# A GRU on one core: stores of the last steps regrouped, and the biases of the last two steps copied into PSUM by VectorE instead of multiplied in by TensorE

## The chip, the core and the metric

The kernel runs on one core of a Trainium2 chip. The metric is the device time of one execution in microseconds (us), lower is better. The core has a matrix engine (TensorE; PE in the profile, with PEld for its weight loads), VectorE (DVE), ScalarE (ACT), GpSimd (POOL) and SyncE (SP). Here SP does no arithmetic: it issues most of the transfers between device memory and the on-chip memory SBUF. Each engine works through its own list of instructions in the order in which the program wrote them; between engines, an instruction waits on semaphores until what it needs is done. Products are added up in PSUM, which is divided into banks of 512 float32 columns on 128 partitions; the kernel uses all eight.

## The reference, cut to what matters

A gated recurrent unit runs over T = 128 steps on a batch of B = 64 with width 512, and its outputs are added to the input:

```python
def step(h, inp):
    x_t, prop = inp
    comb = concatenate([x_t, h], -1)
    z = sigmoid(comb @ Wz + bz)
    r = sigmoid(comb @ Wr + br)
    h_cand = tanh(concatenate([x_t, r * h], -1) @ Wh + bh)
    h_new = (1.0 - z) * h + z * h_cand
    h_next = where(prop, tanh(h_new @ Wp + bp), h_new)   # every fourth step, not the last
    return h_next, h_new
out = x + ys
```

The x parts of the three products depend on no step, the h parts form a chain of 128 steps, and all is float32.

## The kernel before

**Two halves.** The batch is split into two halves of V = 32 rows (`S = 2`). `half(0)` and `half(1)` are generators that write the program; a loop at the end of the file takes turns between them by an estimated cost per product, and so the order of instructions on every engine is written out by that loop (`manual_schedule`: nothing is reordered later). In a step a half goes through its gates R, Z and H, each four units of two products (`gate`). A half's products use two of the four column groups of the matrix engine and 64 of the 128 PSUM partitions, so the two halves run beside each other. I call them lane 0 and lane 1: lane 0 works on partitions 0 to 63, lane 1 on 64 to 127. A step's chain in each lane is: R products, a sigmoid on ACT, `rh` and its transpose `rhT` on DVE, H products, a tanh on ACT, three DVE operations up to the transposed new state `hT`, and the next step's R products. While one of these waits is open, the matrix engine works on Z, on the other lane, and on units of a queue.

**The queue.** `put` appends units of work that is due later (the x products of coming steps), and `fill(n, h)` emits the next n units for lane h at a given place in the program (`PLACES`, `TAIL`, `AT_LAST` hold the counts). Lane 0 and lane 1 each walk the same list. A unit whose function returns `False` is not counted, and the next one is emitted in the same turn. When a list entry has an `end` function, it is called when lane 1 has passed it.

**The last two steps.** Steps T-2 and T-1 (`WIDE = 2`) are computed in another shape (`wide_step`): all x products and biases are added up beforehand in PSUM banks that the earlier method no longer needs, and the h products are added on top. `wide(t, i, h)` names 128 columns for a step, a gate and a half. For T-2 they lie in the banks `scratch_q` (R of both halves, Z of half 1) and `scratch_r` (Z of half 0, H of both); for T-1 in `scratch_a` (R of both, Z of half 1), `scratch_x` (Z of half 0) and `scratch_y` (H). At step T-10 the queue receives the x products of both steps (`wide_unit`, 12 units a step), a unit of bias products after each step's products (`wide_bias`, L595: 12 products for each lane, a 0/1 pattern `picks` times the bias in three bfloat16 parts, `thirds`) and `crossing_unit` (one unit that lane 0 computes for lane 1 and that ACT then copies over to partitions 64 to 127, L588). The first of these products to touch a bank starts the accumulation there.

**Where the units fall.** I follow the queue by hand from the counts: in step T-6 lane 0 emits its first `wide_unit` after `Z` unit 3 and the rest of R and the first two of Z, all of T-2, after its H products; step T-5 takes the rest of Z, H of T-2, the bias unit and the crossing; T-4 takes R and the first half of H of T-1; T-3 takes the rest of H, and Z; the last bias unit falls at the start of T-2 (`AT_LAST`: five units for lane 0, three for lane 1).

**Stores.** `behind_step` adds a step's state to `xr`, which holds four steps of x, on POOL (L968), and stores finished groups of four steps with eight transfers on SP (L978). For the last four steps, three are stored together behind step T-2 (`n = 3 if t == T - 2`), and the last step is stored by `wide_step`: half 0 with one transfer on SP (L1045), half 1 with four, two on SP and two on ACT (L1050).

Of the kernel before, what the change touches and what calls it, by code (L numbers as in the profile page):

```python
# [9 lines left out]
F32 = mybir.dt.float32  # L10
# [8 lines left out]
def kernel(  # L19
# [14 lines left out]
    nc = tc.nc  # L34
    B, T, D = x.shape
# [60 lines left out]
    def part(q):  # L96
        return slice(q * V, (q + 1) * V)
# [427 lines left out]
    def wide(t, i, h):  # L525
        if t == T - 1 and i == H_:
            return scratch[wide_banks(t, i)[0]][:, ts(h, J)]
        n, bank = divmod(ORDER.index((i, h)), 2)
        return scratch[wide_bank(t) + bank][:, ts(n, J)]

    def wide_banks(t, i):
        if t == T - 1 and i == H_:
            return (x_banks[1],)
        return wide_bank(t), wide_bank(t) + 1

    crossing = scratch[x_banks[1]][:, S * J :].rearrange("p (h j) -> p h j", h=S)

    def wide_products(t, i, h, lane, left, w, start=False):
        for c in range(2):
            q = 2 * lane + c  # L540
            nc.tensor.matmul(  # L541
                wide(t, i, h)[part(q)],
                lhsT=left,
                rhs=w[:, ts(q, J)],
                start=start,
                stop=True,
                skip_group_check=True,
            )
# [6 lines left out]
    def x_left(t, h, k):  # L555
        g, j = divmod(t, Q4)
        c0, s0 = divmod(k, C)
        return xT[g][:, j][:, c0, s0 * B + h * V : s0 * B + (h + 1) * V]

    def wide_unit(t, i, k):  # L560
        crossed_one = t == T - 1 and i == H_

        def unit(lane):
            if crossed_one and k == 0 and lane == 1:
                return False
            for h in range(S):
                start = not crossed_one and i != H_ and h == 0 and k == 0
                wide_products(t, i, h, lane, x_left(t, h, k), wx[:, k, i], start)

        return unit, S * J, wide_banks(t, i), None, ()  # L570

    def crossing_unit():
        def unit(lane):
            if lane == 1:
                return False
            for h in range(S):
                for c in range(2):
                    nc.tensor.matmul(
                        crossing[part(c), h],
                        lhsT=x_left(T - 1, h, 0),  # L580
                        rhs=wx[:, 0, H_, ts(2 + c, J)],
                        start=h == 0,
                        stop=True,
                        skip_group_check=True,
                    )

        def end():
            nc.scalar.copy(  # L588
                scratch[x_banks[1]][2 * V :, : S * J].rearrange("p (h j) -> p h j", h=S),
                crossing[: 2 * V],  # L590
            )

        return unit, S * J, (x_banks[1],), end, ()

    def wide_bias(t):  # L595
        def unit(lane):
            for i, row in ((R, 0), (H_, 1), (Z, 2)):
                for h in range(S):
                    for c in range(2):
                        q = 2 * lane + c  # L600
                        nc.tensor.matmul(
                            wide(t, i, h)[part(q)],
                            lhsT=picks[:, q],
                            rhs=thirds[:, row],
                            start=False,
                            stop=True,
                            skip_group_check=True,
                        )

        return unit, 192, wide_banks(t, R) + wide_banks(t, H_), None, ()  # L610

    MB = {}

# [240 lines left out]
    def begin(t):  # L854
        u = (t - 3) % 8
        even = FIRST + 2 * ((t - 3) // 8)
        if t == 1:
            put(batch((1, 0), [(1, 1), (1, 2)]))
        elif t == 2:
            put(batch((1, 1), [(1, 10), (1, 11)]) + batch((1, 2), [(1, 8), (1, 9)]))  # L860
        elif t == 3:
            put(batches(FIRST))
        elif u == 7:
            put(batches(even + 2))
        if t == T - 10:
            put(
                batch((LAST, 0), [(LAST - 1, 4), (LAST, 1)])
                + batch((LAST, 1), [(LAST, 2), (LAST, 10)])
                + [wide_unit(T - 2, i, k) for i in (R, Z, H_) for k in range(K)]
                + [wide_bias(T - 2), crossing_unit()]  # L870
                + [wide_unit(T - 1, i, k) for i in (R, H_, Z) for k in range(K)]
                + [wide_bias(T - 1)]
            )

    def behind_r(t, duo, u):
# [32 lines left out]
    def behind_step(t, duo, u, h_new):  # L908
        g, j = divmod(t, Q4)
        even, odd = FIRST + 2 * duo, FIRST + 2 * duo + 1  # L910
        if t == T - 7:
            pair_left(0, 1, 2, LAST)
            pair_right(0, 1, 10, LAST)
        if t == 0:
            sum_outer(2)
            sum_outer(4)
        if t == 3:
            pair_left(1, 8, 9)
            pair_right(1, 8, 11)

        if duo >= 0:
            if u == 0 and duo >= 1 and odd - 2 < LAST:
                outer_c22(odd - 2)
                outer_c21(odd - 2)
            if even * Q4 < T:
                if u == 0:
                    sum_s34(even)
                elif u == 1:
                    outer_1(even)
                    outer_c11(even)  # L930
                    sum_raw12(odd)
                elif u == 2:
                    sum_raw4(even)
                    outer_u1(even)
                    outer_5(even)
                elif u == 3:
                    outer_c12(even)
                    outer_u2(even)
                    outer_c22(even)
                    if odd < LAST:  # L940
                        sum_s12(odd)
                elif u == 4:
                    if odd < LAST:
# [12 lines left out]
        for i, v in ((0, kept_h[0]), (1, kept_h[1])) if t == 2 else ():  # L956
            o = xr[0][:, i].rearrange("p h (e k) -> p h e k", k=K)
            nc.gpsimd.tensor_add(o, o, v.rearrange("p h (k e) -> p h e k", k=K))
        if duo >= -1 and (even + 2) * Q4 < T:
            if t == 2 or (u == 6 and duo >= 0):  # L960
                sum_raw12(even + 2)
            if u == 7:
                sum_s12(even + 2)
        if t < 2:
            kept_h[t] = h_new
        if 2 <= t < T - 1:
            o = xr[g][:, j].rearrange("p h (e k) -> p h e k", k=K)
            nc.gpsimd.tensor_add(o, o, h_new.rearrange("p h (k e) -> p h e k", k=K))  # L968

        n = 0  # L970
        if t >= T - CHUNK:
            n = 3 if t == T - 2 else 0
        elif j == Q4 - 1:
            n = 4
        if n:
            for h in range(S):
                for q in range(NQ):
                    nc.sync.dma_start(  # L978
                        out=out[ts(h, V), t - n + 1 : t + 1, ts(q, J)],
                        in_=xr[g][part(q), j - n + 1 : j + 1, h, :],  # L980
                    )
# [12 lines left out]
    r_wide = rec[2][:, 1, 0]  # L994
# [6 lines left out]
    def wide_step(t, lane):  # L1001
# [8 lines left out]
        for i, h in ORDER:  # L1010
# [23 lines left out]
            else:  # L1034
# [7 lines left out]
                    continue  # L1042
                nc.vector.tensor_add(o, z_h, o)
                if h == 0:
                    nc.sync.dma_start(  # L1045
                        out=out[ts(h, V), t, :].rearrange("b (q n) -> q b n", q=NQ), in_=o
                    )
                else:
                    for q in (0, 2, 1, 3):
                        both_queues[q // 2].dma_start(out=out[ts(h, V), t, ts(q, J)], in_=o[part(q)])  # L1050

    def half(h):

# [159 lines left out]
```

## Time and profile before

| what | value |
|---|---|
| median of 3 runs | 1258.22 us (1257.46 to 1258.62) |
| the profiled execution, its own time | 1257.26 us |
| its span, first to last instruction | 1255.1 us |
| PE busy | 1247.5 us, 99% |
| DVE, ACT, POOL busy | 64%, 66%, 72% |
| granted TensorE clock, mean | 0.999 |

The profile gives times in us from the start of the span. L541 is line 541 of the kernel. An arrow in a group's name points from the operands to the result. A line of the timeline holds the start, the length, the engine, the line, the operation, the tiles and shapes, the number of instructions merged, and in brackets the idle time in front with the instruction that ended it. L246 is the line of all products of the usual steps, L541 of those of the last two steps, and L284 that of every transpose on DVE. A busy PE is not a measure of how full the array is: instructions of the two lanes overlap, and a record's length contains the way through the array.

### The profile page before, as it was taken

The page shows a single profiled execution, that of the slowest core. Times are in us where ns is not written, and L with a number is a line of the kernel's source. Part 1 is how long each engine was busy: PE and PEld are TensorE (multiplying, and loading weights), DVE is VectorE, ACT ScalarE, POOL GpSimd, SP SyncE. Part 2 cuts the span into 40 slices and gives each one's busy share as a digit, 9 for nine tenths or more (in the row PEclk, how much of TensorE's full clock was granted, in tenths as well). Part 3 has the DMA queues.
Part 4 walks back from the last instruction along what each step waited for, and adds up shares of the span by engine and source line. Part 5 has one row for each costly group of instructions (what it writes and reads, how often), then busy time and mean ns, then how long its engine had stood idle before and what let it go on. Part 6 is the DMA issues. An engine that isn't in the chain of part 4 may idle for free.

```text
span 1255.1 us, 61567 instructions
## 1 busy us (share of the span) xinstructions
PE 1247.5 (99%) x26384; PEld 1180.2 (94%) x26384; DVE 805.9 (64%) x2177; ACT 830.1 (66%) x2666; POOL 908.8 (72%) x1032
## 2 busy tenths in 40 slices
PE   9999999999999999999999999999999999999998
PEld 5999999999999999999999999999999999999987
DVE  5666666666666666666666666666666666666554
ACT  2566666666666676666666666666676666676663
POOL 4988777677876778767778677786777787677530
PEclk9999999999999999999999999999999999999999
DMA  7311112111121110121211211111211111111011
GB/s 249 91 38 40 49 36 53 40 50 42 31 53 52 38 51 24 51 54 37 53 31 41 53 47 43 36 49 41 54 37 46 44 37 53 43 48 36 9 35 33
DMA packets 112292, 61.14 MB, mean 49 GB/s; under 512 B 12776, under 2 KB 109300, under 8 KB 112020
## 3 DMA queue, kind: packets, MB, share of 16 engines
q1 hardware_dynamic: 111588, 56.90, 16.7%
q8 instruction: 208, 3.41, 1.1%
q14 instruction: 64, 0.52, 0.1%
q0 software_dynamic: 256, 0.14, 0.0%
q10 hardware_dynamic: 176, 0.16, 0.0%
HBM read 40.38 MB, written 16.78 MB: 46 GB/s over the span
## 4 chain that ended last, share of the span: by engine, by line
PE 98%; DMA 1%; SPq 0%; DVE 0%; issue 0%; ACT 0%
PE rec L246 44%; PE rec_z L246 16%; PE scratch_r L246 13%; PE scratch_q L246 10%; PE scratch_a L246 5%; PE scratch_y L246 4%; PE scratch_x L246 4%; DMA wx<-in_L_cond_Wh_dram 1%; PE scratch_a L541 0%; PE scratch_q L541 0%; PE scratch_r L541 0%; PE scratch_y L541 0%; SPq L127 0%; PE scratch_x L541 0%; SPq L141 0%
## 5 line engine op out<-in xcount | busy, mean ns | idle before, releaser
L246 PE MATMUL rec<-wh,rhT 128*32 128x256 f32 x4032 | 370.1, 379 | 0.0
L246 PE MATMUL rec<-wh,hT 128*32 128x256 f32 x3008 | 276.6, 379 | 0.0
L246 PE MATMUL rec_z<-wh,hT 128*32 128x256 f32 x3008 | 276.3, 379 | 0.0
L246 PEld LDWEIGHTS rec<-wh,rhT 128*32 128x32 f32 x4032 | 248.5, 110 | 15.8 <-ACT rec L442 0.3
L281 ACT ACTIVATE scratch_r<-rec 64x128 f32<-64x128 f32 x504 | 126.0, 250 | 128.7 <-PE rec L246 63.0
L442 ACT COPY rec<-cp 64x256 f32<-64x256 f32 x504 | 186.8, 371 | 20.2 <-DVE cp L483 1.0
L246 PEld LDWEIGHTS rec_z<-wh,hT 128*32 128x32 f32 x3008 | 191.6, 110 | 5.2
L246 PEld LDWEIGHTS rec<-wh,hT 128*32 128x32 f32 x3008 | 185.0, 110 | 10.4 <-issue 0.8
L281 ACT ACTIVATE rec_z<-rec_z 64x128 f32<-64x128 f32 x488 | 122.0, 250 | 91.1 <-PE rec_z L246 79.5
L281 ACT ACTIVATE c<-rec 64x128 f32<-64x128 f32 x504 | 136.7, 271 | 61.5 <-PE rec L246 50.4
L968 POOL TENSOR_TENSOR xr<-xr,h 128x256 f32<-128x256 f32 x125 | 109.2, 874 | 86.0 <-DVE h L1133 74.4
L711 POOL TENSOR_TENSOR cp<-mb,mb 128x768 f32<-128x768 f32 x76 | 139.0, 1829 | 9.3 <-DVE mb L677 5.6
L711 POOL TENSOR_TENSOR mb<-mb,mb 128x768 f32<-128x768 f32 x58 | 106.2, 1831 | 45.8 <-DVE mb L677 45.8
L711 POOL TENSOR_TENSOR cp<-mb 128x768 f32<-128x768 f32 x46 | 84.3, 1832 | 56.8 <-ACT rec_z L442 55.4
L246 PE MATMUL scratch_r<-tw,s 128*32 128x192 f32 x928 | 120.9, 326 | 0.0
L650 ACT COPY cq<-scratch_q 128x384 f32<-128x384 f32 x212 | 102.1, 482 | 19.5 <-PE scratch_q L246 18.0
L667 DVE TENSOR_TENSOR cx<-scratch_r,cx 128x384 f32<-128x384 f32 x106 | 59.1, 557 | 84.5 <-PE scratch_r L246 69.0
L246 PE MATMUL scratch_q<-tt,s 128*32 128x192 f32 x928 | 103.6, 326 | 0.0
L1097 DVE SCALAR_TENSOR_TENSOR keep<-rec_z,h 128x256 f32<-128x256 f32 x91 | 38.6, 424 | 95.6 <-ACT rec_z L281 86.2
L673 DVE TENSOR_TENSOR mb<-scratch_q,cx 128x384 f32<-128x384 f32 x106 | 59.0, 557 | 62.5 <-ACT cq L650 62.5
L1076 DVE TENSOR_TENSOR rh<-scratch_r,h 128x128 f32<-128x128 f32 x188 | 54.8, 292 | 58.9 <-ACT scratch_r L281 58.9
L246 PE MATMUL rec<-wp,hT 128*32 128x256 f32 x992 | 91.4, 379 | 0.0
(250 smaller groups left out, 3907.3 us busy)
## 6 DMA issues: line engine op xcount, KB each, us to landing
out_dram<-xr SPq DMA_DIRECT2D x249, 64.0 KB, 1.8
xr<-in_x_dram SPq DMA_DIRECT2D x248, 64.0 KB, 2.1
xs<-in_x_dram SPq DMA_DIRECT2D x240, 64.0 KB, 2.0
wx<-in_L_cond_Wz_dram SPq DMA_DIRECT2D x2, 512.0 KB, 7.0
wx<-in_L_cond_Wh_dram SPq DMA_DIRECT2D x2, 512.0 KB, 9.3
wh<-in_L_cond_Wr_dram SPq DMA_DIRECT2D x2, 512.0 KB, 8.3
wh<-in_L_cond_Wz_dram SPq DMA_DIRECT2D x2, 512.0 KB, 5.0
wh<-in_L_cond_Wh_dram SPq DMA_DIRECT2D x2, 512.0 KB, 8.3
```

Source lines behind the costliest of these rows:

```text
L246: nc.tensor.matmul(ps[part(2 * h + c)], lhsT=left, rhs=rhs(c), start=start, stop=True, skip_group_check=True,)
L281: nc.scalar.activation(o, v, func)
L442: nc.scalar.copy(gate_ps(i, h)[rows].rearrange("p d (c n) -> p d c n", c=C), G[t][rows, :, :, i, :].rearrange("p c d n -> p d c n"),)
L650: nc.scalar.copy(c[:, :nm], ps[:, :nm])
L667: nc.vector.tensor_add(T2[what][:, :nm], r_ps[:, :nm], T2[what][:, :nm])
L673: nc.vector.tensor_add(blocks(1, 1), runs(q_ps[:, :nm]), runs(T2[what][:, :nm]))
L711: nc.gpsimd.tensor_add(dst, a, b)
L968: nc.gpsimd.tensor_add(o, o, h_new.rearrange("p h (k e) -> p h e k", k=K))
L1076: nc.vector.tensor_mul(rh[:, h, :], r_, h_old[:, h, :])
L1097: nc.vector.scalar_tensor_tensor(out=kept[0], in0=kept[1], scalar=1.0, in1=kept[2], op0=ALU.subtract, op1=ALU.mult,)
```

## The change

Four things change.

1. **Biases of the last two steps.** At step 64, `load_bias_q` loads the biases br, bz, bh into SBUF tiles `bias_q`, each quarter spread over 32 partitions, with 12 transfers on SP. The bias products (`wide_bias`) go. Instead, queue entries `wide_seeds(t, i)` copy the bias of a gate into the PSUM columns of both halves with two VectorE copies (128 partitions by 128 columns; for H of T-1 only partitions 0 to 63). They are emitted when lane 0 reaches them, and count for nothing in the queue. All products then add to what is there (`start=False`).
2. **The order in the queue.** The seeds stand one gate ahead of their products; R and Z of T-2 stand together at the front. For H of T-1, four bias products in lane 1 remain (`crossing_bias`), and lane 0 skips that entry.
3. **The crossing.** Its two halves go to the last 128 columns of `scratch_y` and `scratch_a`, not both to `scratch_y`, and ACT copies them with two instructions instead of one.
4. **Stores.** Steps T-4 and T-3 are stored together behind T-3 with eight transfers; T-2 with one transfer for each half; of the last step, half 1 goes with one transfer on SP and one on ACT instead of two each.

```diff
@@ wide_unit, crossing_unit
-    crossing = scratch[x_banks[1]][:, S * J :].rearrange("p (h j) -> p h j", h=S)
+    crossing = [scratch[b][: 2 * V, 3 * J :] for b in (x_banks[1], a_bank)]
...
-                start = not crossed_one and i != H_ and h == 0 and k == 0
-                wide_products(t, i, h, lane, x_left(t, h, k), wx[:, k, i], start)
+                wide_products(t, i, h, lane, x_left(t, h, k), wx[:, k, i])
...
-            nc.scalar.copy(
-                scratch[x_banks[1]][2 * V :, : S * J].rearrange("p (h j) -> p h j", h=S),
-                crossing[: 2 * V],
-            )
-        return unit, S * J, (x_banks[1],), end, ()
-    def wide_bias(t):
+            for h in range(S):
+                nc.scalar.copy(wide(T - 1, H_, h)[2 * V :], crossing[h])
+        return unit, S * J, (x_banks[1], a_bank), end, ()
+    def load_bias_q():
+        for n in range(2):
+            tile_ = one.tile([P, S, J], F32, tag=f"h{n}", name=f"bias_q{n}")
+            for i in ((R, Z), (H_,))[n]:
+                bias_q[i] = tile_[:, i % 2]
+        for i, b in ((R, br), (Z, bz), (H_, bh)):
+            for q in range(NQ):
+                nc.sync.dma_start(
+                    out=bias_q[i][part(q)],
+                    in_=b.rearrange("(q o j) -> q o j", q=NQ, o=1)[q].broadcast_to([V, J]),
+                )
+    def wide_seeds(t, i):
         def unit(lane):
+            if lane == 0:
                 for h in range(S):
+                    rows = slice(0, 2 * V) if t == T - 1 and i == H_ else slice(None)
+                    nc.vector.tensor_copy(wide(t, i, h)[rows], bias_q[i][rows])
+            return False
+        return unit, 0, wide_banks(t, i), None, ()
+    def crossing_bias():
+        def unit(lane):
+            if lane == 0:
+                return False
+            for h in range(S):
+                for c in range(2):
+                    nc.tensor.matmul(wide(T - 1, H_, h)[part(2 + c)], lhsT=picks[:, 2 + c],
+                        rhs=thirds[:, 1], start=False, stop=True, skip_group_check=True)
+        return unit, 64, wide_banks(T - 1, H_), None, ()
@@ begin, at T - 10
-                + [wide_unit(T - 2, i, k) for i in (R, Z, H_) for k in range(K)]
-                + [wide_bias(T - 2), crossing_unit()]
-                + [wide_unit(T - 1, i, k) for i in (R, H_, Z) for k in range(K)]
-                + [wide_bias(T - 1)]
+                + [wide_seeds(T - 2, R), wide_seeds(T - 2, Z)]
+                + [wide_unit(T - 2, R, k) for k in range(K)]
+                + [wide_seeds(T - 2, H_)]
+                + [wide_unit(T - 2, Z, k) for k in range(K)]
+                + [wide_seeds(T - 1, R)]
+                + [wide_unit(T - 2, H_, k) for k in range(K)]
+                + [wide_seeds(T - 1, H_), crossing_unit()]
+                + [wide_unit(T - 1, R, k) for k in range(K)]
+                + [wide_seeds(T - 1, Z)]
+                + [wide_unit(T - 1, H_, k) for k in range(K)]
+                + [crossing_bias()]
+                + [wide_unit(T - 1, Z, k) for k in range(K)]
@@ behind_step
-            n = 3 if t == T - 2 else 0
+            n = 2 if t == T - 3 else 0
+            if t == T - 2:
+                for h in range(S):
+                    store_step(t, h)
...
+        if t == T // 2:
+            load_bias_q()
...
+    def store_step(t, h):
+        g, j = divmod(t, Q4)
+        nc.sync.dma_start(
+            out=out[ts(h, V), t, :].rearrange("b (q n) -> q b n", q=NQ), in_=xr[g][:, j, h, :]
+        )
@@ wide_step, the last step
-                    for q in (0, 2, 1, 3):
-                        both_queues[q // 2].dma_start(out=out[ts(h, V), t, ts(q, J)], in_=o[part(q)])
+                    for d in range(2):
+                        both_queues[d].dma_start(
+                            out=out[ts(h, V), t, ts(d, 2 * J)].rearrange("b (q n) -> q b n", q=2),
+                            in_=o[ts(d, 2 * V)],
+                        )
```

More of the change, by code (lines that the diff above doesn't have):

```diff
@@ L578, in unit @@
                     nc.tensor.matmul(
-                        crossing[part(c), h],
+                        crossing[h][part(c)],
                         lhsT=x_left(T - 1, h, 0),
                         rhs=wx[:, 0, H_, ts(2 + c, J)],
-                        start=h == 0,
+                        start=False,
                         stop=True,
@@ L587, in end @@
         def end():
[L588 to L595 removed]
+            for h in range(S):
+                nc.scalar.copy(wide(T - 1, H_, h)[2 * V :], crossing[h])
+        return unit, S * J, (x_banks[1], a_bank), end, ()
+    bias_q = {}
+    def load_bias_q():
[9 more added lines that the diff above has]
+                )
@@ L596, in unit @@
+    def wide_seeds(t, i):
         def unit(lane):
-            for i, row in ((R, 0), (H_, 1), (Z, 2)):
+            if lane == 0:
                 for h in range(S):
[L599 to L608, printed above, removed]
@@ L610, in wide_bias @@
-        return unit, 192, wide_banks(t, R) + wide_banks(t, H_), None, ()
+                    rows = slice(0, 2 * V) if t == T - 1 and i == H_ else slice(None)
[8 more added lines that the diff above has]
+                for c in range(2):
+                    nc.tensor.matmul(
+                        wide(T - 1, H_, h)[part(2 + c)],
+                        lhsT=picks[:, 2 + c],
+                        rhs=thirds[:, 1],
+                        start=False,
+                        stop=True,
+                        skip_group_check=True,
+                    )
+        return unit, 64, wide_banks(T - 1, H_), None, ()
@@ L1044, in wide_step @@
                 if h == 0:
-                    nc.sync.dma_start(
-                        out=out[ts(h, V), t, :].rearrange("b (q n) -> q b n", q=NQ), in_=o
-                    )
-                else:
-                    for q in (0, 2, 1, 3):
-                        both_queues[q // 2].dma_start(out=out[ts(h, V), t, ts(q, J)], in_=o[part(q)])
+                    store_step(t, h)
+                else:
+                    for d in range(2):
+                        both_queues[d].dma_start(
+                            out=out[ts(h, V), t, ts(d, 2 * J)].rearrange("b (q n) -> q b n", q=2),
+                            in_=o[ts(d, 2 * V)],
+                        )
     def half(h):
```

## The prediction

> **What bounds the kernel now.** I read the page first, engines and chain.
>
> ```profile
> PE 1247.5 (99%) x26384; PEld 1180.2 (94%) x26384; DVE 805.9 (64%) x2177; ACT 830.1 (66%) x2666; POOL 908.8 (72%) x1032
> PE 98%; DMA 1%; SPq 0%; DVE 0%; issue 0%; ACT 0%
> ```
>
> The matrix engine is the chain: time in which it stands still is lost for good, and time taken off the others counts only where PE waits for them. The change touches the last seven steps, so next I read windows there (columns: PE, PEld, DVE, ACT, POOL, clock).
>
> ```profile
> 1206.50:1212.00 5.50, 5.50 (x153) 5.28 (x149) 3.31 (x11) 3.55 (x13) 5.34 (x4) 1.00 0.01 3
> 1238.00:1243.00 5.00, 5.00 (x190) 4.77 (x179) 3.02 (x12) 1.35 (x5) 0.88 (x1) 1.00 0.01 3
> 1249.00:1252.00 3.00, 0.00 (x0) 0.00 (x0) 0.72 (x3) 0.24 (x1) 0.00 (x0) 1.00 0.33 82
> ```
>
> PE has no hole up to 1243; behind 1249 only stores remain. The second row prices a queue unit: 190 records in 5.00 us are 0.026 us each, so 8 records in either lane side by side (16) take 0.42 us.
>
> **Part 1: bias products removed.** Lane 0's bias unit of T-2 runs from the first row below to the second.
>
> ```profile
> 1220.72 0.28 PE L601 MATMUL scratch_q<-thirds,picks 96*32 96x128 bf16 x4
> 1221.06 0.28 PE L578 MATMUL scratch_y<-wx,xT 128*32 128x128 f32 x2
> ```
>
> So 0.34 us a lane and step, 0.68 us in all (lane 1 keeps a third of one). Does it shorten the path? Step T-2 begins with R products that need `hT` of T-3:
>
> ```profile
> 1235.80 0.55 ACT L281 ACTIVATE c<-rec 64x128 f32<-64x128 f32 x2 [0.94 <-PE rec L246]
> 1237.17 0.31 DVE L284 STREAM_TRANSPOSE hT<-h 128x128 f32<-128x128 f32 x1
> 1237.70 0.30 PE L541 MATMUL scratch_q<-wh,hT 128*32 128x128 f32 x2
> 1242.72 0.31 DVE L284 STREAM_TRANSPOSE hT<-h 128x128 f32<-128x128 f32 x1
> 1243.09 0.11 PEld L541 LDWEIGHTS scratch_a<-wh,hT 128*32 128x32 f32 x2 [0.21 <-DVE hT L284]
> ```
>
> The last two rows give the step from DVE to PE: 1243.03 to 1243.09, 0.06 us. So `hT`, ready at 1237.48, would have let PE start at 1237.54, and it started at 1237.70: slack 0.16. Following the queue by hand, lane 0 has four x units and a bias unit between its H products and this place now, and three x units after the change, because the entries taken out move all others forward. The 0.34 of T-2's bias is spent on one more unit (0.42) ahead of the H products, +0.08, and the start can then come only 0.16 earlier. I take -0.1 us, not -0.68; bounds 0 and -0.7.
>
> **Part 2: the seeds, where PE must wait.** A seed is emitted directly ahead of lane 0's next unit, behind whatever DVE was given before. In T-6 the seeds of R and Z stand behind `rhT` of half 1 and ahead of the first x unit:
>
> ```profile
> 1206.70 0.39 PE L541 MATMUL scratch_q<-wx,xT 128*32 128x128 f32 x4
> 1207.09 0.41 PE L246 MATMUL rec_z<-wh,hT 128*32 128x256 f32 x2
> 1207.66 0.31 DVE L284 STREAM_TRANSPOSE rhT<-rh 128x128 f32<-128x128 f32 x1
> 1209.32 0.42 DVE L1097 SCALAR_TENSOR_TENSOR keep<-rec_z,h 128x256 f32<-128x256 f32 x1 [1.34 <-ACT rec_z L281]
> ```
>
> PE comes to that unit at 1206.70; DVE cannot copy before 1207.97. No copy of this shape is in the trace; the nearest rows, the columns being mean ns after the busy time:
>
> ```profile
> L311 DVE COPY xT<-scratch_y 128x256 f32<-128x256 f32 x1 | 0.4, 426 | 2.8 <-PE scratch_y L306 2.8
> L363 DVE TENSOR_TENSOR tt<-tt,wx 128x256 f32<-128x256 f32 x2 | 0.9, 426 | 0.1
> L363 DVE TENSOR_TENSOR tt<-tt,wx 128x128 f32<-128x128 f32 x2 | 0.6, 292 | 0.1
> L67 DVE MEMSET zeros<- 128x256 uint32 x1 | 0.3, 272 | 0.9 <-PEq L1199 0.9
> ```
>
> A copy costs what an addition does at 256 columns, so I take 0.29 us at 128; the memset (272 ns for 256 words) makes 0.15 the lower bound, the 426 ns row the upper. Neighbours on DVE overlap by 0.07 (the T-4 rows below), so the pitch is 0.22. Which of the four copies does PE wait for? Semaphores here follow the bank, not the columns:
>
> ```profile
> ACT scratch_r L281 <- DVE mb L676: 50.5, 44, 1.1
> ACT z L281 <- PE rec_z L246: 1.6, 2, 0.8
> 1215.99 0.55 ACT L281 ACTIVATE z<-rec_z 64x128 f32<-64x128 f32 x2 [0.79 <-PE rec_z L246]
> ```
>
> In the first, ACT writes columns 384 to 511 of `scratch_r` and waits 44 times for DVE's read of columns 0 to 383. In the last, ACT reads partitions 0 to 63 of `rec_z` and yet waits until lane 1's products into the others end. The fourth copy (Z of half 1) lies in `scratch_q` too, so PE waits for all four: 1207.90 + 3 x 0.22 + 0.29 + 0.06 = 1208.91. Lane 0 stands still from 1206.70 (2.2 us). PE's list being in order, lane 1's next products (1207.09) stand behind it (1.8 us). **A: +2.0 us.**
>
> **B.** Later in T-6 the seeds of H (bank `scratch_r`) stand behind `hT` of half 1 and ahead of the first Z unit, same bank:
>
> ```profile
> 1210.19 0.27 PE L541 MATMUL scratch_r<-wx,xT 128*32 128x128 f32 x1
> 1211.60 0.31 DVE L284 STREAM_TRANSPOSE hT<-h 128x128 f32<-128x128 f32 x1
> ```
>
> 1211.84 + 0.22 + 0.29 + 0.06 = 1212.41 against 1210.19: 2.2, less the 0.4 that lane 0 lost beyond lane 1 at A. **+1.8 us.**
>
> **C.** The seeds of R of T-1 in T-5 lie in `scratch_a`, which PE does not touch until later; the two copies push `keep` by 0.4 us into DVE's idle time. **0**; up to 0.3 if `hT` of half 1 gets late.
>
> **D.** The seeds of H of T-1 stand behind `hpT` of half 0, ahead of the crossing, both in `scratch_y`:
>
> ```profile
> 1221.10 0.31 DVE L284 STREAM_TRANSPOSE hpT<-hprop 128x128 f32<-128x128 f32 x1 [1.43 <-ACT hprop L281]
> 1221.78 0.56 ACT L281 ACTIVATE hprop<-rec 64x128 f32<-64x128 f32 x2 [0.31 <-PE rec L246]
> 1222.36 0.37 ACT L442 COPY rec<-cp 64x256 f32<-64x256 f32 x1
> 1222.76 0.34 ACT L588 COPY scratch_y<-scratch_y 64x256 f32<-64x256 f32 x1
> 1221.54 0.31 PE L541 MATMUL scratch_r<-wx,xT 128*32 128x128 f32 x2
> ```
>
> 1221.34 + 0.51 + 0.06 = 1221.91; the crossing is due where the bias stood, 1220.72: 1.2 in lane 0, some 0.85 in lane 1. **+1.1 us.**
>
> **D2.** ACT's copy of the crossing now also reads `scratch_a`, and the next unit of R in lane 1 writes that bank. ACT comes to it 1.0 us after the second tanh pair starts (1221.78 to 1222.76) and needs two instructions, about 0.55 by a pair of 64x128 (that row: 0.56 for two). Lane 1's next unit begins 0.24 ahead of that tanh (1221.54), so PE resumes 0.24 + 0.98 + 0.56 + 0.06 = 1.84 us after it, with work for 0.42 (lane 1) to 0.8 us (lane 0). **+1.1 us**, bounds 0 and 1.4: by partitions the two do not meet, but the `rec_z` row says that does not help.
>
> Here the Trainium skill speaks the other way: "PSUM — Partial Sum Buffer", in its section on bank collisions, says that two engines may use one bank at once when they are in different quadrants of 32 partitions. By that D2 need not exist, and the sum would be 1.1 us lower; the `rec_z` row, a wait of 0.79 us across quadrants, does not agree, and I keep D2.
>
> **E.** In T-4 the seeds of Z of T-1 (`scratch_x`, `scratch_a`) stand behind `hT` of half 0; lane 1's last R unit (`scratch_a`) follows:
>
> ```profile
> 1228.65 0.27 PE L541 MATMUL scratch_y<-wx,xT 128*32 128x128 f32 x1
> 1228.86 0.31 DVE L284 STREAM_TRANSPOSE hT<-h 128x128 f32<-128x128 f32 x1
> 1229.10 0.25 DVE L1097 SCALAR_TENSOR_TENSOR keep<-z,hprop 128x128 f32<-128x128 f32 x1
> ```
>
> 1229.10 + 0.51 + 0.06 = 1229.67; lane 0's unit behind it is due at 1228.65. **+1.05 us.**
>
> **Part 3: mid-run loads.** 12 transfers; SP needs 4.89 us for eight stores:
>
> ```profile
> 654.61 4.54 SPq L978 DMA_DIRECT2D out_dram<-xr  x8
> 660.73 4.77 SPq L102 DMA_DIRECT2D xr<-in_x_dram  x8
> 1245.47 4.89 SPq L978 DMA_DIRECT2D out_dram<-xr  x8
> 1249.60 0.29 DVE L1043 TENSOR_TENSOR xr<-z,xr 128x128 f32<-128x128 f32 x1
> 1250.46 0.70 SPq L1045 DMA_DIRECT2D out_dram<-xr  x1
> 1251.27 0.82 SPq L1050 DMA_DIRECT2D out_dram<-xr  x2
> ```
>
> So 7 us in a stretch where SP idles 1.6 us (659.15 to 660.73): the next x load comes up to 6 us later, and is needed three steps later, about 30 us by 1255 / 128 = 9.8 a step. That hides it: **0**; if not, up to 6.
>
> **Part 4: stores at the end.** Now SP is at eight old stores until 1250.36, and issues the last one by 1252.09, 2.2 us after the result is there (1249.89). After the change the eight go out behind T-3, and SP has 0.41 (16 KB) to 0.70 us (64 KB) of issue left for 32 KB: 1250.3 to 1250.6. **-1.6 us** (-1.4 to -1.8).
>
> **Sum.** 2.0 + 1.8 + 1.1 + 1.1 + 1.05 = 7.05; -0.1 - 1.6 gives +5.35 us. The profiled execution took 1257.26 (span 1255.1 and 2.2 around it), 0.96 less than the median 1258.22; on the median: 1263.6 us, 0.43% slower. With the lower copy price (0.15; two overlapping at 0.08) the 10 copies that count are 1.4 us cheaper, with the upper (0.43, at 0.36) 1.4 dearer: 1262.2 to 1265.0; without D2, 1262.5. Own range 1261 to 1266.
>
> **Rivals.** *Seeds cost nothing* (other side): if semaphores went by columns, PE would wait only at A, and there for two copies. The place is the bank; decisive are 4.2 us of waits (1.7 gained plus 2.5, which is 0.2%, about what a measurement of this kernel tells from no change): below them it is no slower. With A alone at 1.5, 1258.1; with none, 1256.5. Against it speak the 44 waits above. *The clock falls*: PE stands still for about 2 us twice within 6.
>
> ```profile
> 1252.50:1255.00 2.50, 0.00 (x0) 0.00 (x0) 0.00 (x0) 0.00 (x0) 0.00 (x0) 0.50 0.05 12
> ```
>
> Behind the last products (1249) the clock is still 1.00 until 1252 and 0.50 later: it needs 3 us of idleness, longer than any wait here. If it did fall for 3 us, 1.5 us are added: 1265.1. The Trainium skill, "TensorE: Matmul & The Clock Gate", section on oscillation, likewise warns of idle gaps over about 3.4 us; the trace agrees with 3 us. *SP late*: if the loads held x up by their 6 us, 1269.
>
> **How the numbers follow.** Forecast, with or without D2: 0.76. Seeds free or nearly: 0.13, within 0.2% in 0.11 of it and faster in 0.02. Clock: 0.07. SP: 0.04. Predicted is the forecast's 1263.6. The range leaves out SP and the part of the free-seeds case under 1258: 1258.0 to 1267.0. Slower: 0.76 + 0.07 + 0.04, less 0.01 for a forecast with every bound low, 0.86; same 0.12; faster 0.02.
>
> **What would show it.** Right: PE idle ahead of L541 at `scratch_q` and `scratch_r` in T-6, released by DVE copies, about 2 us each; 1 us at `scratch_y` in T-5 and T-4; an ACT release at `scratch_a`; SP's last issue within 1 us of L1043's end. Wrong: PE without holes between 1206 and 1243, or products of the other lane overtaking a waiting one.

## The result, and the profile after the change

The changed kernel takes 1265.53 us in the median of 6 runs (1263.74 to 1267.02), the kernel before, run beside it, 1257.80: a ratio of 1.0061, 95% interval 1.0050 to 1.0071. It is slower by 0.6%. The profiled execution of the changed kernel took 1263.86 us, with a span of 1261.7 us against 1255.1 before.

The page of the changed kernel, engines and chain:

```profile
PE 1248.9 (99%) x26340; PEld 1171.8 (93%) x26340; DVE 808.9 (64%) x2189; ACT 830.9 (66%) x2667; POOL 909.2 (72%) x1032
PE 97%; DMA 1%; DVE 1%; ACT 1%; SPq 0%; issue 0%; DVEq 0%; ACTq 0%
```

DVE has 12 instructions more, PE 44 less, and a mean over 1261 us shows nothing else. The windows around T-6 do (columns: PE, PEld, DVE, ACT, POOL, clock):

```profile
1206.50:1212.00 5.50, 3.76 (x85) 3.02 (x83) 2.40 (x9) 2.47 (x10) 5.34 (x4) 1.00 0.00 0
1212.00:1214.50 2.50, 0.75 (x28) 0.48 (x25) 1.99 (x8) 0.92 (x3) 2.50 (x3) 1.00 0.02 7
```

In the first window PE was busy for 5.50 of 5.50 us before the change, with 153 products; now it is busy for 3.76, with 85. PE stands still in a stretch where it had no hole, and the clock stays at 1.00. What it waits for stands in the groups of waits of the matrix engine from 1195 us on (in us: total, times, longest), first the five longest of the weight loads and then all of the products:

```profile
PEld scratch_q L541 <- issue: 2.2, 1, 2.2
PEld scratch_r L541 <- DVE scratch_r L611: 2.0, 1, 2.0
PEld scratch_a L541 <- ACT scratch_y L588: 1.2, 1, 1.2
PEld scratch_y L577 <- DVE scratch_y L611: 1.1, 1, 1.1
PEld scratch_a L541 <- DVE scratch_a L611: 1.1, 1, 1.1
```

```profile
PE scratch_r L541 <- DVE scratch_r L611: 1.7, 1, 1.7
PE scratch_q L541 <- DVE scratch_q L611: 1.7, 1, 1.7
PE scratch_a L541 <- DVE scratch_a L611: 0.8, 1, 0.8
PE scratch_a L541 <- ACT scratch_y L588: 0.8, 1, 0.8
PE scratch_y L577 <- DVE scratch_y L611: 0.7, 1, 0.7
```

Five waits, each once. L611 is the copy of a seed, L588 ACT's copy of the crossing. The first wait is put down to "issue" for the weight loads; the products' row names what released it, the seed in `scratch_q`. The timeline shows each at its place:

```profile
1207.15 0.29 DVE L1117 TENSOR_TENSOR rh<-scratch_r,h 128x128 f32<-128x128 f32 x1 [0.32 <-ACT scratch_r L281]
1208.40 0.28 DVE L611 COPY scratch_q<-bias_q 128x128 f32<-128x128 f32 x1
1208.83 0.30 PE L541 MATMUL scratch_q<-wx,xT 128*32 128x128 f32 x2 [1.74 <-DVE scratch_q L611]
1212.54 0.31 DVE L284 STREAM_TRANSPOSE hT<-h 128x128 f32<-128x128 f32 x1
1213.40 0.31 DVE L284 STREAM_TRANSPOSE hT<-h 128x128 f32<-128x128 f32 x1
1214.29 0.30 PE L541 MATMUL scratch_r<-wx,xT 128*32 128x128 f32 x2 [1.75 <-DVE scratch_r L611]
1217.69 0.29 DVE L1117 TENSOR_TENSOR rh<-scratch_r,h 128x128 f32<-128x128 f32 x1 [3.46 <-ACT scratch_r L281]
1218.65 0.29 DVE L1117 TENSOR_TENSOR rh<-scratch_r,h 128x128 f32<-128x128 f32 x1 [0.32 <-ACT scratch_r L281]
1225.41 0.31 DVE L284 STREAM_TRANSPOSE hpT<-hprop 128x128 f32<-128x128 f32 x1 [1.43 <-ACT hprop L281]
1226.28 0.30 PE L577 MATMUL scratch_y<-wx,xT 128*32 128x128 f32 x2 [0.66 <-DVE scratch_y L611]
1227.58 0.31 DVE L284 STREAM_TRANSPOSE hpT<-hprop 128x128 f32<-128x128 f32 x1 [1.36 <-ACT hprop L281]
1228.54 0.30 PE L541 MATMUL scratch_a<-wx,xT 128*32 128x128 f32 x2 [0.76 <-ACT scratch_y L588]
1230.68 0.29 DVE L1117 TENSOR_TENSOR rh<-scratch_r,hprop 128x128 f32<-128x128 f32 x1 [2.79 <-ACT scratch_r L281]
1236.05 0.30 PE L541 MATMUL scratch_a<-wx,xT 128*32 128x128 f32 x2 [0.78 <-DVE scratch_a L611]
1244.68 0.31 DVE L284 STREAM_TRANSPOSE hT<-h 128x128 f32<-128x128 f32 x1
1256.95 0.29 DVE L1083 TENSOR_TENSOR xr<-z,xr 128x128 f32<-128x128 f32 x1
```

The DVE rows are events that both kernels have, so they measure what each wait cost the recurrence. The rows of before that answer to them and were not shown yet:

```profile
1207.33 0.29 DVE L1076 TENSOR_TENSOR rh<-scratch_r,h 128x128 f32<-128x128 f32 x1 [0.32 <-ACT scratch_r L281]
1210.62 0.31 DVE L284 STREAM_TRANSPOSE hT<-h 128x128 f32<-128x128 f32 x1
1213.59 0.29 DVE L1076 TENSOR_TENSOR rh<-scratch_r,h 128x128 f32<-128x128 f32 x1 [1.68 <-ACT scratch_r L281]
1214.83 0.29 DVE L1076 TENSOR_TENSOR rh<-scratch_r,h 128x128 f32<-128x128 f32 x1 [0.60 <-ACT scratch_r L281]
1222.37 0.31 DVE L284 STREAM_TRANSPOSE hpT<-hprop 128x128 f32<-128x128 f32 x1 [0.96 <-ACT hprop L281]
1224.23 0.29 DVE L1076 TENSOR_TENSOR rh<-scratch_r,hprop 128x128 f32<-128x128 f32 x1 [1.55 <-ACT scratch_r L281]
```

At the first row the changed kernel is 0.18 us ahead (1207.15 against 1207.33). Each later event less its row of before, plus this 0.18, is what has been lost by then, and the difference between neighbours belongs to what lies between them:

| event of both kernels | lost so far, us | step of the prediction between | predicted | measured |
|---|---|---|---|---|
| `hT` of half 1, T-6 (1211.60, 1213.40) | 1.98 | A | 2.0 | 1.98 |
| `rh` of half 0, T-5 (1213.59, 1217.69) | 4.28 | B | 1.8 | 2.30 |
| `hpT` of half 0, T-5 (1221.10, 1225.41) | 4.49 | C | 0 | 0.21 |
| `hpT` of half 1, T-5 (1222.37, 1227.58) | 5.39 | D | 1.1 | 0.90 |
| `rh` of half 0, T-4 (1224.23, 1230.68) | 6.63 | D2 | 1.1 | 1.24 |
| `hT` of half 0, T-3 (1237.17, 1244.68) | 7.69 | E | 1.05 | 1.06 |
| last addition (1249.60, 1256.95) | 7.53 | part 1 | -0.1 | -0.16 |

Between its first two rows the table passes from lane 1 to lane 0. Within a lane, A cost 2.10 us in lane 0 (`hT` of half 0 in T-6, 1210.62 to 1212.54) and 1.98 in lane 1; B then cost 2.18 us in lane 0 and 2.02 in lane 1 (`rh` of half 1 in T-5, 1214.83 to 1218.65, has lost 4.00). Behind C both lanes have lost 4.49 us: `hT` of half 1 in T-5 moved from 1219.36 to 1223.67.

The path through the last seven steps is 7.53 us longer. Behind the last addition stands the end: before, 1249.89 to 1255.07, 5.18 us; now 1257.24 to 1261.69, 4.45 us, 0.73 us less. From the first step's `rh` to T-6 there is no loss, 1183.80 us against 1183.96. So 7.53 - 0.73 - 0.18 = 6.62 us, which is the 6.6 us between the profiled executions. The medians are 7.7 us apart, 1.1 us more; the runs of either kernel scatter by 1.5 to 3.3 us, and that remainder is not resolved.

### The profile page after: what moved, and what is told of

Its sections match the earlier page's. It is cut to its first block, busy times and chain, and to the rows that moved or that the text cites. A ratio compares the mean times of both kernels' runs of the same rounds, so it can differ in the third digit from the quotient of the medians.

```text
span 1261.7 us, 61495 instructions
## 1 busy us (share of the span) xinstructions
PE 1248.9 (99%) x26340; PEld 1171.8 (93%) x26340; DVE 808.9 (64%) x2189; ACT 830.9 (66%) x2667; POOL 909.2 (72%) x1032
## 4 chain that ended last, share of the span: by engine, by line
PE 97%; DMA 1%; DVE 1%; ACT 1%; SPq 0%; issue 0%; DVEq 0%; ACTq 0%
PE rec L246 44%; PE rec_z L246 16%; PE scratch_r L246 13%; PE scratch_q L246 10%; PE scratch_a L246 5%; PE scratch_y L246 4%; PE scratch_x L246 4%; DMA wx<-in_L_cond_Wh_dram 1%; PE scratch_a L541 0%; PE scratch_r L541 0%; PE scratch_q L541 0%; SPq L127 0%; PE scratch_y L541 0%; ACT c L281 0%; PE scratch_x L541 0%
```

## The experiments

The theory: PE's list is in order, and five entries in it now wait for a copy that an engine could not give earlier; that costs 7 us, and the stores give back 1.6. Its rivals: the holes have another cause than the copies (the loads, the products taken out, an entry moved); the waits go by columns or partitions rather than banks; the stores' gain was lost to something else.

In the readings below, "the path" is the time from the start of `rh` of half 1 in T-6 to the start of the last addition: 42.27 us before (1207.33 to 1249.60) and 49.80 after (1207.15 to 1256.95). "The end" runs from the end of that addition to the end of the span.

**The changed kernel again.** No edit.

> The changed kernel once more, for its ratio beside the others and a second trace. Theory W: from rh of half 1 in T-6 to the last result 50.1 us again; what differs between its executions lies ahead of the first step or behind the last result, not in the holes. Rival V (the holes vary): that stretch differs by over 1 us between the two traces.

Measured: 1265.14 us in 5 runs, ratio 1.0060 (1.0048 to 1.0073); its path is again 49.80 us and its end 4.46. What follows is compared at this grain: the tail of the changed kernel repeated to 0.01 us in two executions, while the start of an execution does not (see the last section).

**Stores alone.** Part 4 put into the kernel before, with no change of the biases:

```diff
-            n = 3 if t == T - 2 else 0
+            n = 2 if t == T - 3 else 0
+            if t == T - 2:
+                for h in range(S):
+                    store_step(t, h)
...
-                    for q in (0, 2, 1, 3):
-                        both_queues[q // 2].dma_start(out=out[ts(h, V), t, ts(q, J)], in_=o[part(q)])
+                    for d in range(2):
+                        both_queues[d].dma_start(
+                            out=out[ts(h, V), t, ts(d, 2 * J)].rearrange("b (q n) -> q b n", q=2),
+                            in_=o[ts(d, 2 * V)],
+                        )
```

> The kernel before with part 4 alone (stores regrouped, no change to the biases). Theory W (PE waits for the seeds; the stores only help): 0.7 us under the kernel before if the ACT issue of 1.37 us in the profile after comes again, 1.6 under it if that issue takes some 0.5 us as forecast. Rival S (the stores are part of the loss): above the kernel before.

Measured: 1257.38 us, ratio 1.0000 (0.9991 to 1.0008). The end is 5.06 us instead of 5.18. Neither 1.6 nor 0.7 us are gained, but 0.1. The timeline and SP's own waits say where it went; first the kernel with the stores alone:

```profile
1249.36 0.29 DVE L1052 TENSOR_TENSOR xr<-z,xr 128x128 f32<-128x128 f32 x1
1249.68 0.53 SPq L1059 DMA_DIRECT2D out_dram<-xr  x1
1249.68 1.36 ACTq L1059 DMA_DIRECT2D out_dram<-xr  x1
```

```profile
SPq L1220 <- DMA out_dram<-xr: 2.8, 1, 2.8
```

and the same wait of the kernel before (total, times, longest):

```profile
SPq L1208 <- DMA out_dram<-xr: 1.2, 1, 1.2
```

SP's part went as predicted: its last issue ends 0.56 us after the result (1249.65 to 1250.21) and not 2.2 us. But SP then waits 2.8 us for a landing where it waited 1.2: 1.6 us gained and 1.6 us lost. What is late next is the transfer itself. ACT's 32 KB take 1.36 us to issue, and the last landing in the trace is 3.35 us after the result (3.36 in the changed kernel), where before it was 3.48.

**The size of the last transfers.** The regrouping of T-4 to T-2 is kept, and the last step goes out in the four 16 KB transfers of before; the diff is the one above without its second half.

> The kernel before with the stores of T-4 to T-2 regrouped as in the change, but the last step of half 1 stored in four transfers of 16 KB as before. Theory E (what was gained on SP is lost on ACT, whose one transfer of 32 KB takes 1.37 us to issue where two of 16 KB take 0.8): the last landing comes 2.6 to 2.8 us behind the last result instead of 3.4, 0.7 us less than in e1_stores_only. Rival: no difference, 3.3 us or more.

Measured: 1256.05 us in 11 runs, ratio 0.9984 (0.9976 to 0.9993), the only kernel here that beats the one before. Its end in the timeline:

```profile
1249.90 0.29 DVE L1052 TENSOR_TENSOR xr<-z,xr 128x128 f32<-128x128 f32 x1
1250.22 0.85 ACTq L1059 DMA_DIRECT2D out_dram<-xr  x2
1250.22 0.80 SPq L1059 DMA_DIRECT2D out_dram<-xr  x2
```

Two transfers on each queue are issued in 0.80 and 0.85 us, the last one lands in the trace 2.09 us after the result, 0.5 us sooner than the theory had it, and the end is 3.67 us, 1.5 us less than before. So clearing SP's backlog was worth what the prediction said of part 4; making two transfers of four took it away again.

**Is it ACT's slow issue, or the shape?** The kernel with the stores alone, with both 32 KB transfers on SP:

```diff
-                        both_queues[d].dma_start(
+                        nc.sync.dma_start(
```

> e1_stores_only with both 32 KB transfers of the last step issued by SP. Theory E (ACT's issue of 1.37 us is what holds the last landing): SP issues them in 0.53 us each, the last lands 2.9 to 3.1 us behind the last result instead of 3.35. Rival P (transfers of this shape land late whoever issues them, as SP's landed 2.5 us behind its start): 3.0 us or more and no gain over e1_stores_only that can be told.

Measured: 1257.62 us, ratio 0.9999 (0.9989 to 1.0008); last landing 3.21 us after the result, end 4.85.

```profile
1250.78 0.29 DVE L1052 TENSOR_TENSOR xr<-z,xr 128x128 f32<-128x128 f32 x1
1251.10 1.10 SPq L1059 DMA_DIRECT2D out_dram<-xr  x2
```

The timeline shows SP issuing both in 1.10 us, 0.26 sooner than ACT issued its one, and the landing is 0.15 us earlier than the 3.36 of the changed kernel. From the end of the last issue to the last landing it takes 2.1 us here, 2.0 with the stores alone and 1.2 with four transfers of 16 KB. So the queue is not the main thing, as the rival had it; a 32 KB transfer over two row blocks lands late from either. Why is not settled.

**Biases alone.** The changed kernel with the stores of before:

```diff
-            n = 2 if t == T - 3 else 0
-            if t == T - 2:
-                for h in range(S):
-                    store_step(t, h)
+            n = 3 if t == T - 2 else 0
...
+                    for q in (0, 2, 1, 3):
+                        both_queues[q // 2].dma_start(out=out[ts(h, V), t, ts(q, J)], in_=o[part(q)])
```

> The changed kernel with the stores of before. Theory W: the last result (end of the last addition into xr) stays at about 1257.2, 7.35 later than before, and the span ends 5.2 us behind it: about 1262.4, 7.4 us above the kernel before in all. Rival S: less than 5 us above it.

Measured: 1266.37 us in 4 runs, ratio 1.0064 (1.0049 to 1.0080). From `rh` of T-6 to the first `rh` of T-2 it takes 39.63 us, the changed kernel 39.62 and the one before 32.09, so the whole loss of the path is in the biases. The medians are 8.7 us apart, where 7.4 was expected, and two things came as a surprise. Its end is 4.43 us, as short as the changed kernel's, with the stores of before. And behind T-2 its path is 0.7 us longer, by a wait that the changed kernel has not:

```profile
PEld scratch_y L541 <- issue: 0.6, 1, 0.6
```

**The copies themselves.** The changed kernel without the twelve copies; entries, loads and stores stay.

```diff
-                    nc.vector.tensor_copy(wide(t, i, h)[rows], bias_q[i][rows])
+                    pass
```

> The changed kernel without the ten VectorE copies that PE waits for (and the two of step T-5 that it does not): the biases of the last two steps are left out but for four products, all else is as in the changed kernel, the mid-run loads too. Theory W: the holes at scratch_q and scratch_r in T-6, at scratch_y in T-5 and at scratch_a in T-4 close, the one behind ACT's copy of the crossing (1.2 us) stays, the last result comes some 0.9 to 1.2 us later than before, and the time is within 0.6 us of the kernel before. Rival Q (the shorter queue or the loads cost the time): still 5 us or more above the kernel before.

Measured: 1259.58 us, ratio 1.0014 (1.0005 to 1.0023). The profiled execution took 1257.09 us, within the expectation; the median did not, as the nine other runs lie at 1259.2 to 1260.7; why they do is not shown. The path is 43.58 us (1206.66 to 1250.24): of the 7.53 us, 6.22 are gone. The products' waits for L611 are gone with them, and one is left:

```profile
PE scratch_a L541 <- ACT scratch_y L588: 1.1, 1, 1.1
```

That is D2. The copies cost 6.2 us, and D2, together with whatever else moved, 1.3.

**D2 by itself.** The crossing's second bank becomes `scratch_x` in place of `scratch_a`; the seeds stay.

```diff
-    crossing = [scratch[b][: 2 * V, 3 * J :] for b in (x_banks[1], a_bank)]
+    crossing = [scratch[b][: 2 * V, 3 * J :] for b in (x_banks[1], x_banks[0])]
...
-        return unit, S * J, (x_banks[1], a_bank), end, ()
+        return unit, S * J, (x_banks[1], x_banks[0]), end, ()
```

> The changed kernel with the second half of the crossing in scratch_x instead of scratch_a; nothing else is changed. Theory W (semaphores go by the bank): the wait for ACT's copy at scratch_a is gone and the kernel is 1.2 us faster than the changed one, some 6.2 to 6.5 us above the kernel before; the four holes behind VectorE stay. Rival A (PE waits for ACT wherever the crossing lies): no faster than the changed kernel.

Measured: 1264.40 us in 4 runs, ratio 1.0052 (1.0038 to 1.0066). The ACT release at `scratch_a` is not among the waits any more, and up to the first `rh` of T-2 the kernel is 0.99 us quicker than the changed one (38.63 against 39.62). The path as a whole gains only 0.13 (49.67): the wait that the kernel with the biases alone showed stands here too.

```profile
PEld scratch_y L541 <- issue: 0.8, 1, 0.8
```

**Seeds where DVE has time.** All six seeds are taken out of PE's list and emitted right behind `join` of half 1 in T-6 and T-5, before PE's next entry needs the bank; with it the edit of D2, and the x unit that T-6 ran between these places goes later (its count in the table TAIL from 1 to 0).

```diff
-        T - 10: (6, 8, 0), T - 9: (1, 7, 5), T - 8: (1, 7, 0), T - 7: (0, 6, 0), T - 6: (1, 5, 0),
+        T - 10: (6, 8, 0), T - 9: (1, 7, 5), T - 8: (1, 7, 0), T - 7: (0, 6, 0), T - 6: (0, 6, 0),
...
                 join(t, duo, u, 0)
+                if t in (T - 6, T - 5):
+                    for i in (R, Z, H_):
+                        wide_seeds(t + 4 if t == T - 6 else T - 1, i)[0](0)
```

> The changed kernel, with all seeds of T-2 copied behind rhT of half 1 in T-6 and all of T-1 at the same place in T-5, where VectorE sat idle for over 1 us; lane 0's first x unit of T-6 moved behind the H products; the crossing's second half in scratch_x. Theory W (only the place of the copies in VectorE's list costs time): all five holes close; from rh of half 1 in T-6 to the last result some 42.6 to 43.3 us (before 42.56, changed 50.09), the rest being lane 0's wait of up to 0.45 us for rhT in T-6 and the shorter queue; the kernel is 7 us faster than the changed one. Rival C (the copies themselves cost, wherever they stand): 46 us or more.

Measured: 1257.64 us in 11 runs, ratio 0.9999 (0.9989 to 1.0008). The twelve copies are all there, and the path is 42.66 us (1207.35 to 1250.01), 0.39 more than before: 7.1 of the 7.5 us are gone. No wait of the products is left from 1195 us on. Of the weight loads these are the three longest, the first of which the kernel before has too, and the only one for a copy:

```profile
PEld rec L246 <- ACT rec_z L442: 0.4, 1, 0.4
PEld scratch_q L541 <- DVE hT L284: 0.4, 1, 0.4
PEld rec L246 <- ACT scratch_r L281: 0.3, 1, 0.3
PEld scratch_q L541 <- DVE scratch_q L611: 0.2, 1, 0.2
```

So it is not the copy that is dear, but its place. The 7.1 us belong to three edits together, the place of the copies, the crossing's bank and the x unit; the copies' own share is the 6.2 us of the run without them. With these edits the kernel has all four parts of the change, and it draws with the one before.

**One wait put back.** The same with TAIL as it was, so that PE comes to the first x unit of T-2 before the copies can run, as in A.

> As e5_seeds_early, but lane 0's first x unit of T-6 stays ahead of the H products, so it still meets the copies of R and Z there. Theory W: one hole of about 2.0 us at scratch_q in T-6 is back and no other; from rh of half 1 in T-6 to the last result about 44.5 to 45 us.

Measured in one execution: 1258.90 us; path 44.46 us (1207.24 to 1251.70), 1.80 more than with the unit moved, and one wait is back:

```profile
PE scratch_q L541 <- DVE scratch_q L611: 1.7, 1, 1.7
```

A is shown alone, at the size predicted for it to 0.2 us.

**What the products were worth.** The kernel before, with the bias products of both steps left out and their entries kept:

```diff
-            for i, row in ((R, 0), (H_, 1), (Z, 2)):
+            for i, row in ():
```

> The kernel before with the products of both bias units left out (so the biases of the last two steps are missing), their entries kept in the queue. Theory of part 1 (the start of T-2 is bound by hT, not by PE): the bias of T-2 is worth its 0.34 us, that of T-1 only the slack of 0.16: from rh of half 1 in T-6 to the last result 42.56 less 0.5. Rival (PE bound all the way): less 0.68.

Measured in one execution: 1261.55 us, of which 3.6 us are a later first step. From T-6 to the first `rh` of T-2, behind the last of the products left out, it takes 31.81 us, 0.28 less than before (32.09). So by this execution all bias products of both steps are worth 0.28 us, less than the 0.5 expected and than the 0.68 that their records add up to. Behind T-2 this kernel too has the wait by "issue" at `scratch_y`, 0.7 us, and its whole path is longer than before, 42.85 us against 42.27; the expectation for the whole path is missed either way.

**Early seeds and four last transfers.** The two edits that helped, together.

> e5_seeds_early with the last step of half 1 stored in four transfers of 16 KB. Theory E: 0.8 us less behind the last result than in e5_seeds_early (3.7 instead of 4.46), and in all as far above e10_stores_last_four as its steps are longer, 0.4 us: about 1256.8. Rival: the gain of e10_stores_last_four does not carry over.

Measured: 1257.51 us in 11 runs, ratio 1.0000 (0.9991 to 1.0009). The end is 3.02 us, the shortest of all, 2.2 us less than before and 1.4 less than with the early seeds alone, where 0.8 was expected. The path is 43.28 us from `rh` to the last addition, 0.62 longer than with the early seeds and large transfers, and the same wait is back, so in all the gain does not carry over:

```profile
PEld scratch_y L541 <- issue: 0.6, 1, 0.6
```

The better kernel remains the one that only regroups the stores of T-4 to T-2.

## Why the prediction was right, step by step

Direction, mechanism and range held: 1265.53 us lies within 1258.0 to 1267.0, 1.9 us above the 1263.6 predicted.

- **A, D, E** came within 0.2 us of their terms (the rows of E give 1.02, put down as 1.05). Each was an entry of PE's list whose due time stood in a row of before, against a DVE event plus copies; that a copy takes 0.29 us was taken from an addition's row, and the copies of L611 took 0.27 to 0.29.
- **B** was mis-sized: 1.8 predicted, 2.30 in the table, 2.18 and 2.02 within the lanes. The waiting product did resume where the working put it, 0.89 us behind the start of `hT` (1213.40 to 1214.29; predicted 0.81). The step that failed is the subtraction of 0.4 us for what lane 0 had lost beyond lane 1 at A; without it the term is 2.2. Lane 0 had lost 2.10 us at `hT` of T-6 and lane 1 1.98, so the difference was 0.12 and not 0.4.
- **C** was 0 with up to 0.3: 0.21 in lane 0, and 0.49 in lane 1, which had lost less at B.
- **D2** was right in kind and nearly in size (1.24; 1.1 predicted). The run without it removes the wait and 0.99 us. ACT reads partitions 0 to 63 of `scratch_a`, and PE waits although its unit belongs to the other half. The section on bank collisions of the Trainium skill's "PSUM — Partial Sum Buffer" allows such a pair; this program's waits do not go that way, and here the row decided rightly over the rule. Whether the banks themselves would bear it, no run here shows.
- **Part 1** was right: the slack ahead of T-2's R products, 0.16, is what came off there: these products now start at 1245.05, 0.06 behind the end of `hT` (1244.68 + 0.31) and no longer 0.22. In the kernel before, the removal of all the products alone is worth 0.28.
- **Part 3** was right: the twelve loads run on SP from 658.95, the next load of x moves from 660.73 to 665.32, and nothing follows from it.

```profile
658.95 1.84 SPq L601 DMA_DIRECT2D bias_q<-in_L_cond_br_dram  x4
665.32 5.02 SPq L102 DMA_DIRECT2D xr<-in_x_dram  x8
```

- **Part 4** is the step that failed: -1.6 predicted, -0.73 measured in the changed kernel, and -0.1 of it by the stores alone. The working stopped at SP's last issue and took the landing behind it as given. The other -0.6 came with the biases: their kernel with old stores has an end of 4.43 against 5.18, and of each pair with equal stores the one with the biases' change ends 0.6 to 0.75 us sooner (4.45 and 5.06, 3.02 and 3.67). The traces show where: the last landing hardly moved (3.48 us behind the result before, 3.39 with the biases alone, 3.36 in the changed kernel), but from it to the end of the span it takes 1.58 to 1.71 us in the five traces without the biases' change and 0.97 to 1.10 in the eight with it. There SP goes through a list of closing waits, one by one (L1208 before, L1249 after). Seven of them stand behind the last landing before, and one of the steps between them takes 0.36 us; after the change four are left. So this 0.6 us is not the stores' work, and it was luck for the prediction. Why fewer waits are left is not tested; the copies are not the reason, as the kernel without them ends in 4.46.

The sum: the path 0.58 us longer than forecast (B 0.5 by the table), the end 0.87 us longer, 0.18 gained ahead of T-6; that is 1.27 of the 1.9 us. The rest is that the changed kernel's profiled execution lies 1.67 us under its median, where 0.96 was allowed for.

Of the rivals, *seeds cost nothing* is refuted: PE waited at five places, and in T-6 until 0.15 us behind the end of the fourth copy. *The clock falls* is refuted: every window above stands at 1.00 through holes of 2.2 us, and the granted clock stays there until 1258.98, behind the last product. *SP late* did not occur.

## What to carry to other kernels

A cheap copy that takes the place of cheap products is judged by when its engine can run it, not by its 0.28 us: in an in-order list the first product that needs it holds up everything behind it, in both lanes. Compare each moved operation's earliest start on the new engine with the due time of the first entry that touches the bank, and emit it a stage earlier if that fails; here the copies at their late place were 6.2 of 7.5 us, and 7.1 came back with an earlier place for them and another bank for the crossing. And follow a store to its landing: after a shorter issue comes the transfer, and fewer, larger transfers at the very end landed later here.

## What the runs showed of the hardware that was not expected

- ACT took 1.36 to 1.38 us to issue one 32 KB transfer over two row blocks, SP 0.53 to 0.55; two of 16 KB took SP 0.80 to 0.83 (with the biases alone 1.02) and ACT 0.83 to 0.87. The last landing came 3.2 to 3.4 us after the result with 32 KB, and 2.05 to 2.09 us with 16 KB where SP had no older stores left to issue.
- The first step starts at different times in executions that do the same: `rh` of T = 0 stood at 23.37 us before, 22.81 without the copies and 26.99 without the bias products, and the granted clock opened after 6.19 us before and after 9.59 us with the biases alone; without the bias products it fell back to 0.50 from 11.61 to 15.02 us. In the middle the executions agree within 0.2 us (1183.79 to 1183.96), so a tail is better compared from its own first event than from the start of the span.

```profile
22.81 0.29 DVE L1117 TENSOR_TENSOR rh<-scratch_r,h_init 128x128 f32<-128x128 f32 x1 [0.41 <-ACT scratch_r L281]
```

```profile
26.99 0.29 DVE L1076 TENSOR_TENSOR rh<-scratch_r,h_init 128x128 f32<-128x128 f32 x1 [1.56 <-ACT scratch_r L281]
```

- In four of the twelve traces taken besides the one before, PE stood for 0.6 to 0.8 us amid the products of `scratch_y` in T-1 with nothing named as the reason. They are not the kernels with seeds (one has none), nor those with one kind of stores. The packed traces point to PE's own instructions. In all four PE stops at the same place of its list, ahead of record 53185 or 53186 (products, weight loads and waits counted together), and goes on 1.22 to 1.48 us after the end of a 16 KB packet of queue q8, whose 208 packets are marked as instructions. In the other nine traces PE passes that place without a stop, 1.59 to 2.04 us after the end of such a packet. So PE probably waits there for its next block of instructions; no run here moves such a block, and so the cause is argued, not shown. The wait is worth as much as most of what was tried here.
